# Two reorderings in an attention kernel: a small subtraction moved from VectorE to GpSimd in batch 1, and a large subtraction and its exponential moved behind two sums in five batches

## The chip, the cores and the metric

The kernel runs on one core of one Trainium2 chip. The time is the device time of one execution in microseconds (us). TensorE (PE) multiplies, VectorE (DVE) and GpSimd (POOL) do elementwise work and reductions, ScalarE (ACT) copies and takes exponentials, SyncE (SP) issues most of the DMAs. Each engine works through its own list of instructions in the order in which they were issued to it, and waits where an operand or a buffer is not ready.

## The reference, cut to what matters

All data are float32: `x` is 16 x 100 x 640, the context 16 x 722 x 384, of which the last 4 positions are the "tokens" `ca` and the other 718 are `enc`. There are 8 heads of 80.

```python
query = hidden_states @ Wq
keyt = enc @ Wk
valt = enc @ Wv
hs = _mha(query, keyt, valt)                       # large attention, 100 x 718 per head
ca_q1 = jnp.einsum('btc,th->bch', ca, Wq_ca)
ca_q1 = ca_q1[:, indices, :]
ca_hs1 = _mha(ca_q1, residual, residual)           # first softmax of the token path
ca_q2 = ca_hs1 @ Wq
ca_k2 = ca @ Wk_ca
ca_v2 = ca @ Wv_ca
ca_hs2 = _mha(ca_q2, ca_k2, ca_v2)                 # second softmax, over 4 tokens
out = hs + ca_hs2
out = out @ Wout + b_out
out = out + residual
```

## The kernel before, in words

A loop over the 16 batches `b` does, in each turn, the scores and the softmax of the large attention for batch `b`, the keys for batch `b + 1` and the values for batch `b`, the second softmax of the token path for `b`, the scores of the first softmax of the token path for `b + 1`, and the output projection of an earlier pair of row chunks. The order of all instructions on all engines is written out by hand (`tc.manual_schedule`, so the order in the source is the order on each engine).

**Keys and values.** The products of `enc` with `Wk` and `Wv` are cut into 15 products each, on sums and differences of blocks of `enc` and of the weights (class `Blocks`, lines 385 to 405; `Values`, product on line 431; `Keys`, product on line 462). `V_PLAN` and `K_PLAN` list the products: each adds into a PSUM bank (A, B, C, D or E, shown as `v_psA`, `k_psB` and so on), and after it the bank as it then stands is read into one block of the result. The first product for a block of the result is copied by ACT (line 404), every later one is added by DVE (line 402). Banks keep adding up, so the next product into a bank has to wait until the bank was read. `vv.go(n)` and `kk.go(n)` issue the next `n` values or keys products with their reads. Bank C of the values consists of two PSUM tiles, and gets the plan's products 8 and 10. Product 8 is copied by ACT; product 10 is added by DVE in two instructions of 120 x 320. `k_psC`, the bank of the keys' product 10, is opened later, in the PSUM pool that holds the two tiles of `v_psC`.

**Large softmax.** The scores lie in three tiles `st[0]` to `st[2]` of 120 x 1600. `Maximum` (lines 856 to 907) finds each row's maximum `over`; `subtract(i)` (line 1517, DVE, both inputs in SBUF) takes it off a tile and `exponential(i)` (line 1525, ACT) follows. In the middle batches the order is: values products 8 and 9, keys product 8, `subtract(0)`, `exponential(0)`, values product 10, `subtract(1)`, values 11, keys 9 and 10, `exponential(1)`, values 12, keys 11 and 12, values 13, keys 13, values 14, keys 14, `subtract(2)`, `exponential(2)`. On ACT the copy of keys product 9 (`kT<-k_psB`) thus stands behind `exponential(0)`, and on DVE the sum of values product 11 (`vs<-v_psB`) behind `subtract(1)`.

**Token path.** `scores1` (lines 972 to 990) makes the scores of the first softmax on POOL: for each of the 4 tokens a product (line 980), and from the second on an addition into `e1` (line 987). `scores2` takes two reductions on DVE (lines 1053 and 1060) and then the subtraction of the tokens' maximum, 100 x 32, on line 1062, on the engine that the caller names: DVE in batches 0 and 1, POOL in all others. `exponentials2` (1068, ACT), `softmax3` (1073 and 1074 on DVE, 1076 on POOL) and `values2` (POOL: products 1091, additions 1098; each product reads a tile `vb` that a DMA of SP fills) end the path.

**Output batches.** For `last.b in PAIRS`, that is in batches 3, 6, 8, 11 and 13, two chunks of 128 output rows are projected. `last.load` (line 1133, POOL) adds the bias onto the two tiles `xn` of the residual, `last.sums` (line 1240, POOL) forms two sums of the transposed rows, and `project_pair` does the products (line 1259, PE) and adds what they give to `xn` (line 1270, DVE); its first product is read before its bank takes the third. In the odd ones of these batches (3, 11, 13) a transposition of the token path (line 872, DVE, 128 x 800) is issued ahead of the first such read, in 6 and 8 behind it. The three tail instructions of POOL ahead of `values2` in these batches are thus: product 1076, the two sums of 1240.

Of the kernel before, what the change touches and what calls it, by code (L numbers as in the profile page):

```python
# [16 lines left out]
CAD, T = 384, 4  # L17
# [21 lines left out]
PAIRS = {ENDS[r + 1]: r for r in range(0, 10, 2)}  # L39
# [80 lines left out]
def kernel(  # L120
# [18 lines left out]
    nc = tc.nc  # L139
# [67 lines left out]
    def load_enc(b):  # L207
        enc = enc_tile(f"enc_{b}"), None
        for u, lo, hi in ((0, 0, 3), (1, 1, 3), (2, 0, 2)):
            at = A_RAW[u, lo]  # L210
            nc.sync.dma_start(
                out=enc[0][:, at : at + hi - lo],
                in_=enct[b][:, lo:hi, u * (KT - 1) : u * (KT - 1) + KT],
            )
        return enc

    def load_rest(b, enc):
        if b == 1:
            room = hsT_tile("rest_1").rearrange("p c s -> p (c s)")
            rest = room[:, : len(A_REST) * KT].rearrange("p (i k) -> p i k", k=KT)  # L220
        else:
            rest = rest_tile(f"rest_{b}")
        for (u, c), i in A_REST.items():
            nc.sync.dma_start(
                out=rest[:, i], in_=enct[b][:, c, u * (KT - 1) : u * (KT - 1) + KT]
            )
        return enc[0], rest
# [681 lines left out]
    def load_m(b):  # L909
        if b < 2:  # L910
            return lambda c: m_sb[c][:, b * HT : (b + 1) * HT]
        mb = small.tile([P, HC, HT], F32, tag="mb", name=f"mb_{b}", bufs=2)
        nc.sync.dma_start(
            out=mb, in_=m_d[:, :, b * HT : (b + 1) * HT].rearrange("c p n -> p c n")
        )
        return lambda c: mb[:, c]
# [491 lines left out]
    second = Second(0, xT, ca_0)  # L1408
# [77 lines left out]
    last, enc_next, second_next = None, load_rest(1, load_enc(1)), Second(1, xT)  # L1486
# [8 lines left out]
    for b in range(B):  # L1495
        p = b // 2
        e_in, now = enc, second
        enc, second = enc_next, second_next
# [17 lines left out]
        def subtract(i):  # L1516
            return nc.vector.tensor_tensor(  # L1517
                st[i],
                st[i],
                top.over[:KN].unsqueeze(1).to_broadcast([KN, 2, ROWS]),  # L1520
                ALU.subtract,
            )

        def exponential(i):
            nc.scalar.activation(st[i], st[i], AF.Exp, scale=SCALE)  # L1525

        def larger(i):
            for u in range(2):
                most_now = nc.vector.tensor_tensor(  # L1529
                    most[:KN], most[:KN], st[i][:, u], ALU.max  # L1530
                )
            return most_now
# [19 lines left out]
        seen = larger(2)  # L1552
# [4 lines left out]
        if b == 0:  # L1557
            second.scores1(seen)
            m_next = load_m(b + 2)
            kk.go(3)  # L1560
            top.go(3)
            first_values(3, e_in, (act, act), get=bank)
            top.go(1)
            kk.go(2)
            now.scores2()
            now.exponentials2()
            first_values(0, e_in, (act, act), (0,), bank)
            top.go()
            kk.go(3)
            first_values(0, e_in, (act, act), (1,), bank)  # L1570
            now.softmax3()
            kk.go(2)
            subtract(0)
            exponential(0)
            kk.go(2)
            subtract(1)
            kk.go(3)
            exponential(1)
            second_next, enc_next = loads()
            less = subtract(2)  # L1580
            exponential(2)
            last_keys(b + 1, enc)
            enc_next = load_rest(b + 2, enc_next)
            keys(m_next)
            now.values2(less)
            enc_sums(enc_next)
            second.softmax1(4)
        elif b + 1 < B:
            vv = Values(b, e_in)

            def both(n):
                vv.go(n)
                kk.go(n)

            forms = [wout_sb[:, 2 * i : 2 * i + 2, k * (H // 2) : (k + 1) * (H // 2)]
                     for i in range(2) for k in range(2)]
            if b == 2:
                for o, left, right in (
                    (forms[1], forms[1], forms[0]),
                    (wout2[:, 0], forms[3], forms[1]),  # L1600
                    (wout2[:, 1], forms[2], wout2[:, 0]),
                ):
                    nc.gpsimd.tensor_tensor(o, left, right, ALU.subtract)
            elif last.b - 1 in PAIRS:
                nc.gpsimd.tensor_tensor(wout2[:, 0], wout2[:, 0], forms[0], ALU.add)
            second.scores1(seen, range(T - 1))
            top.go(3)
            kk.go(3)
            vv.go(3)
            now.scores2(nc.vector if b == 1 else nc.gpsimd)  # L1610
            second.scores1(None, range(T - 1, T))
            now.load(behind=seen)
            last.load(seen)
            top.go(1)
            if b > 1:
                last.place()
            now.exponentials2()
            both(2)
            both(2)
            top.go()  # L1620
            both(1)
            now.softmax3()
            if b == 1:
                nc.gpsimd.tensor_tensor(last.hs[:S], last.hs[:S], last.hs2, ALU.add)
            if last.b in PAIRS:
                last.sums()
            later = range(T - 1, T) if b in MIXED or last.b in PAIRS else range(0)
            now.values2(None, range(T - len(later)))
            vv.go(2)
            kk.go(1)  # L1630
            subtract(0)
            exponential(0)
            vv.go(1)
            subtract(1)
            vv.go(1)
            kk.go(2)
            exponential(1)
            vv.go(1)
            kk.go(2)
            both(1)  # L1640
            both(1)
            if b == 1:
                for f in list(wv_there):
                    nc.scalar.copy(wv_sb[:, W_AT[f]], wv_there.pop(f))
            mixed = None
            if b in MIXED:
                second_next, enc_next = loads()
                mixed = Queries(p + 1, xT_at[0], enc_next[0])
                if last.b not in PAIRS:
                    mixed.sums()  # L1650
            if b == 1:
                nc.gpsimd.dma_start(out=bias, in_=bout[0].partition_broadcast(P))
            if not mixed:
                second_next, enc_next = loads()
            if b + 2 < B:
                m_next = load_m(b + 2)
            late = mixed and last.b not in PAIRS
            if not late:
                subtract(2)
            if not late and b not in PLAIN:  # L1660
                exponential(2)
            if b + 2 < B:
                enc_next = load_rest(b + 2, enc_next)
            if b == 1:
                last.transpose()
            if last.b in PAIRS:
                last.project_pair(lambda n: second.softmax1(n, True))
                if last.b == max(PAIRS):
                    nc.sync.dma_start(
                        out=forms[1],  # L1670
                        in_=wout[: 2 * P, H // 2 :].rearrange("(c p) n -> p c n", p=P),
                    )
            if not mixed and last.b in PAIRS:
                now.values2(None, later)
            if b == 1:
                second.softmax1(8)
        else:
            room = enc_tile("spare").rearrange("p f k -> p (f k)")
            spare.extend(room[:, i * H : (i + 1) * H] for i in range(2))
            last.transpose()  # L1680
            vv = Values(b, e_in)
            last.load()
            mine.load()
            now.load(behind=seen)
            top.go(3)
            vv.go(3)
            last.project_few(len(OC) - 2)
            now.scores2(nc.gpsimd)
            now.exponentials2()
            top.go(1)  # L1690
            vv.go(3)
            top.go()
            vv.go(2)
            now.softmax3()
            now.values2()
            vv.go(2)
            subtract(0)
            exponential(0)
            vv.go(5)
            for i in (1, 2):  # L1700
                subtract(i)
                exponential(i)
            last.project()
# [129 lines left out]
        last = mine  # L1833
# [55 lines left out]
```

## Time and profile before

| | before |
|---|---|
| timed runs (3) | 905.66, 906.13, 906.14 us; median 906.13 |
| profiled execution | 907.72 us, of which its span is 906.0 |
| granted TensorE clock | 1.00 |
| instructions in the span | 28486 |
| HBM traffic | 55.59 MB read, 5.57 MB written, 68 GB/s over the span |

The page of the profile gives for each engine its busy time and share; the timeline gives one row for each run of equal instructions: start and duration in us, engine, line of the kernel, operation, written tile <- read tiles with shapes, the count, and in brackets the idle time of the engine ahead of the row and what ended it. A duration of DVE or POOL holds the time that the instruction waited after it was issued. A group's row gives count, shortest, median and longest duration in ns. The waits view adds up who waited for whom (us in total, times, longest).

### The profile page before, as it was taken

Reading aid. Unit: us, or ns where it says so; the run is one execution under the profiler, and the core shown is the slowest. Engines: PE = TensorE matmul, PEld = TensorE weight load, DVE = VectorE, ACT = ScalarE, POOL = GpSimd, SP = SyncE. Lnnn points to the kernel's source line nnn. Section 1 sums busy time; section 2 is a strip of 40 time slices with the busy share of each in tenths; the row PEclk is TensorE's granted clock in tenths of the full one; section 3 lists DMA queues with packets and bytes.
Section 4 is the critical chain, followed back from the end, with each engine's and each line's share of the span. In section 5 each row is a group of like instructions: output and inputs, shape, how many; then the busy total and the mean of one; then the engine's idle time right before and its main releaser. Section 6 shows DMA issues by size and latency. Waiting matters only on the chain.

```text
span 906.0 us, 28486 instructions
## 1 busy us (share of the span) xinstructions
PE 900.3 (99%) x12200; PEld 748.1 (83%) x12200; DVE 720.6 (80%) x1278; ACT 461.9 (51%) x917; POOL 712.8 (79%) x684
## 2 busy tenths in 40 slices
PE   9999999999999999999999999999999999999998
PEld 6898889787797878878798787988879788797866
DVE  3669796999849898786987869788984899848893
ACT  2344543747437564644737446375742747437451
POOL 8689998787868889696896959958897688976633
PEclk9999999999999999999999999999999999999999
DMA  8723111132301212230122301203130031310111
GB/s 292 264 70 92 36 58 43 37 95 53 112 4 52 80 41 67 54 105 32 53 56 53 106 34 52 56 25 107 54 83 32 24 107 53 98 32 24 62 47 38
DMA packets 50627, 63.00 MB, mean 70 GB/s; under 512 B 13594, under 2 KB 37850, under 8 KB 50500
## 3 DMA queue, kind: packets, MB, share of 16 engines
q1 hardware_dynamic: 48852, 59.18, 21.4%
q8 instruction: 96, 1.57, 0.7%
q10 hardware_dynamic: 1024, 1.15, 0.4%
q0 software_dynamic: 624, 0.85, 0.3%
q14 instruction: 31, 0.25, 0.1%
HBM read 55.59 MB, written 5.57 MB: 68 GB/s over the span
## 4 chain that ended last, share of the span: by engine, by line
PE 94%; DVE 5%; ACT 0%; DMA 0%; issue 0%; DVEq 0%
PE a_ps L1806 12%; PE s_ps L781 12%; PE v_psA L431 10%; PE k_psA L462 8%; PE v_psB L431 8%; PE k_psB L462 6%; PE o_ps L1259 5%; PE k_psA L742 4%; PE v_psC L431 3%; PE k_psC L462 3%; PE v_ps L372 2%; PE q_ps L599 2%; PE q_ps L541 2%; PE v_psD L431 2%; PE v_psE L431 2%; PE k_psE L462 1%
## 5 line engine op out<-in xcount | busy, mean ns | idle before, releaser
L980 POOL TENSOR_TENSOR e<-ca,g 100x800 f32<-100x800 f32 x64 | 97.9, 1540 | 90.9 <-ACT kT L404 67.4
L1806 PEld LDWEIGHTS a_ps<-vs,st 120*64 120x64 f32 (+3 forms) x3072 | 119.0, 124 | 10.1 <-issue 0.7
L497 POOL TENSOR_TENSOR enc<-enc 128x240 f32<-128x240 f32 x144 | 113.2, 796 | 14.2 <-DMA enc<-in_enct 7.2
L1806 PE MATMUL a_ps<-vs,st 120*64 120x81 f32 (+3 forms) x3072 | 122.8, 233 | 0.0
L1517 DVE TENSOR_TENSOR st<-st,over 120x1600 f32<-120x1600 f32 x48 | 116.6, 2431 | 0.0
L431 PE MATMUL v_psA<-wv_sb,enc 128*120 128x320 f32 x352 | 109.3, 433 | 0.0
L1098 POOL TENSOR_TENSOR hs<-hs,hs 100x640 f32<-100x640 f32 x48 | 94.8, 1975 | 3.8
L987 POOL TENSOR_TENSOR e<-e,e 100x800 f32<-100x800 f32 x48 | 93.4, 1945 | 3.8
L462 PE MATMUL k_psA<-enc,wk_sb 128*128 128x240 f32 x384 | 95.2, 371 | 0.2 <-DVE kT L402 0.2
L1091 POOL TENSOR_TENSOR hs<-vb,p 100x640 f32<-100x640 f32 x64 | 90.6, 1426 | 3.8 <-DMA vb<-va_d 1.5
L431 PE MATMUL v_psB<-wv_sb,enc 128*120 128x320 f32 x296 | 91.9, 433 | 0.0
L1525 ACT ACTIVATE st<-st 120x1600 f32<-120x1600 f32 x48 | 73.9, 1539 | 23.5 <-DVE st L1517 23.2
L462 PEld LDWEIGHTS k_psA<-enc,wk_sb 128*128 128x128 f32 x384 | 71.5, 190 | 16.4 <-issue 1.2
L431 PEld LDWEIGHTS v_psA<-wv_sb,enc 128*120 128x120 f32 x352 | 64.2, 183 | 25.0 <-DVE vs L402 0.5
L1529 DVE TENSOR_TENSOR most<-most,st 120x800 f32<-120x800 f32 x64 | 68.0, 1063 | 14.3 <-ACT st L831 13.2
L462 PE MATMUL k_psB<-enc,wk_sb 128*128 128x240 f32 x320 | 77.9, 366 | 0.0
L781 PE MATMUL s_ps<-qp,kT 64*56 64x100 f32 (+1 forms) x3072 | 73.3, 248 | 0.0
L431 PEld LDWEIGHTS v_psB<-wv_sb,enc 128*120 128x120 f32 x296 | 54.1, 183 | 21.8 <-DVE vs L402 0.4
L781 PEld LDWEIGHTS s_ps<-qp,kT 64*56 64x56 f32 (+1 forms) x3072 | 67.0, 130 | 5.5 <-issue 4.2
L837 ACT COPY st<-s_ps 120x800 f32<-120x800 f32 x64 | 49.8, 830 | 38.7 <-PE s_ps L781 38.5
L1166 ACT COPY hsT<-turned_hs 32x160 f32<-32x160 f32 (+7 forms) x244 | 67.7, 278 | 3.0
L462 PEld LDWEIGHTS k_psB<-enc,wk_sb 128*128 128x128 f32 x320 | 60.9, 190 | 7.9
(213 smaller groups left out, 1905.9 us busy)
## 6 DMA issues: line engine op xcount, KB each, us to landing
vb<-va_d SPq DMA_DIRECT2D x62, 250.0 KB
enc<-in_enct SPq DMA_DIRECT2D x30, 240.0 KB
enc<-in_enct SPq DMA_DIRECT2D x15, 360.0 KB
xT<-in_xt SPq DMA_DIRECT2D x8, 500.0 KB
rest<-in_enct SPq DMA_DIRECT2D x31, 120.0 KB
xn<-in_x SPq DMA_DIRECT2D x11, 320.0 KB
out<-xn SPq DMA_DIRECT2D x11, 320.0 KB
ca<-in_cas SPq DMA_DIRECT2D x16, 156.2 KB
```

The lines of the kernel that those rows point to most:

```text
L431: nc.tensor.matmul(at[0][j][:KN, : H // 2], a_form(self.enc, f)[:, j * KN : (j + 1) * KN], wv_there.get(f, wv_sb[:, W_AT[f]]), start=first ...
L462: nc.tensor.matmul(at[:, i * KT : (i + 1) * KT], wk_sb[:, W_AT[f], i], a_form(self.enc, f), start=(first and i == 0), stop=last, skip_grou ...
L497: nc.gpsimd.tensor_tensor(out, left, right, op)
L781: nc.tensor.matmul(s_ps[at][k0:k1, cols], w, rhs, start=not begun & {(at, k) for k in range(k0, k1, 32)}, stop=last, skip_group_check=True,)
L980: first = nc.gpsimd.tensor_tensor(to, self.ca[:, t, :].unsqueeze(1).to_broadcast([S, NH, S]), g[:, :, t].unsqueeze(2).to_broadcast([S, NH, ...
L987: made = nc.gpsimd.tensor_tensor(e, e, to, ALU.add)
L1091: first = nc.gpsimd.tensor_tensor(to, self.vb[t][:S].rearrange("p (h d) -> p h d", h=NH), p2[:, :, t].unsqueeze(2).to_broadcast([S, NH, D] ...
L1098: nc.gpsimd.tensor_tensor(sums, sums, to, ALU.add)
L1517: return nc.vector.tensor_tensor(st[i], st[i], top.over[:KN].unsqueeze(1).to_broadcast([KN, 2, ROWS]), ALU.subtract,)
L1525: nc.scalar.activation(st[i], st[i], AF.Exp, scale=SCALE)
L1529: most_now = nc.vector.tensor_tensor(most[:KN], most[:KN], st[i][:, u], ALU.max)
L1806: nc.tensor.matmul(a_v[lo:hi, h % 4], st[i // 2][: KEYS[i], i % 2, h * S + lo : h * S + hi], block(i, h // 4)[: KEYS[i], h % 4], start=(i ...
```

## The change

It edits the middle branch of the loop (batches 1 to 14).

- Batch 1: `scores2` names POOL instead of DVE, and all four tokens of `second.scores1` are issued behind it. Before, three tokens were issued ahead and one behind, and the first one's explicit wait on `seen` (the third score tile's maximum, DVE) stood on the first product; this now holds only for the later batches. On POOL the 100 x 32 subtraction stands ahead of the seven instructions of `scores1`.
- Output batches (3, 6, 8, 11, 13): values product 10 with its two sums is issued ahead of `subtract(0)` and `exponential(0)` instead of behind them. PE's order and ACT's order stay as they are, since PE has nothing in `subtract` and `exponential`, and ACT has nothing in values product 10; on DVE the two sums of bank C (`vs<-v_psC`, line 402) go ahead of the first L1517, which then stands directly ahead of the second.

```diff
-            second.scores1(seen, range(T - 1))
+            if b > 1:
+                second.scores1(seen, range(T - 1))
             top.go(3)
             kk.go(3)
             vv.go(3)
-            now.scores2(nc.vector if b == 1 else nc.gpsimd)
-            second.scores1(None, range(T - 1, T))
+            now.scores2(nc.gpsimd)
+            if b > 1:
+                second.scores1(None, range(T - 1, T))
+            else:
+                second.scores1()
             now.load(behind=seen)
...
             vv.go(2)
             kk.go(1)
+            if last.b in PAIRS:
+                vv.go(1)
             subtract(0)
             exponential(0)
-            vv.go(1)
+            if last.b not in PAIRS:
+                vv.go(1)
             subtract(1)
```

## The prediction

> **What bounds the kernel now.** I read the page first (busy shares and the chain that ended last), then who TensorE waited for, then the timeline of the six places that the diff touches.
>
> ```profile
> PE 900.3 (99%) x12200; PEld 748.1 (83%) x12200; DVE 720.6 (80%) x1278; ACT 461.9 (51%) x917; POOL 712.8 (79%) x684
> ...
> PE 94%; DVE 5%; ACT 0%; DMA 0%; issue 0%; DVEq 0%
> ```
>
> ```profile
> PE k_psC L462 <- DVE vs L402: 0.3, 1, 0.3
> PE k_psA L462 <- DVE kT L402: 0.2, 1, 0.2
> ```
>
> TensorE (PE) is busy for 900.3 of 906.0 us and the chain is 94% PE. Past the start it waits in two places only, both for a sum on VectorE (DVE). So the change can give back tenths, while everything it puts late on DVE, ScalarE (ACT) or GpSimd (POOL) lengthens the run as soon as a PE product waits for it. The question is thus how much slack PE has behind the moved subtraction.
>
> **Part 1, batch 1.** The small subtraction (L1062) goes from DVE to POOL.
>
> ```profile
> 110.52 3.03 POOL L980 TENSOR_TENSOR e<-ca,g 100x800 f32<-100x800 f32 x2
> 110.83 1.28 DVE L1062 TENSOR_TENSOR e<-s,mx 100x32 f32<-100x32 f32 x1
> 114.48 1.05 PE L462 MATMUL k_psA<-enc,wk_sb 128*128 128x240 f32 x4 [0.20 <-DVE kT L402]
> 115.55 1.08 PE L462 MATMUL k_psE<-enc,wk_sb 128*128 128x240 f32 x4
> ```
>
> ```profile
> L1062 POOL TENSOR_TENSOR e<-s,mx x14: 238/243/249, 170.9 to 872.1; 100x32 f32<-100x32 f32 x14
> ```
>
> On DVE it lasts 1.28 us, ending as POOL's first product (half of 3.03) is over; on POOL the same operation takes 0.243 us. DVE gets about 1.2 us back, and its queue behind holds the sums whose lateness stopped PE for 0.20 us at 114.48. With that wait goes the slow restart behind it: k_psE follows k_psA after 1.07 us, where a key block gives way to the next after 0.81 us in batch 8 (506.67 to 507.48, quoted below). I take 0.7 us off (0.2 waited, 0.26 here, the rest in the pauses beside it), between 0.2, the wait alone, and 0.75. POOL now waits for DVE's maximum until some 110.75, so its products start about 0.45 us later, and so does what is queued behind them.
>
> ```profile
> L980 POOL TENSOR_TENSOR e<-ca,g 100x800 f32<-100x800 f32 x64 | 97.9, 1540 | 90.9 <-ACT kT L404 67.4
> ```
>
> POOL stands idle for 90.9 us ahead of such products, nearly 6 us a batch, which takes up the 0.45; without that cover it would delay batch 2's by as much.
>
> **Part 2, batches 3, 6, 8, 11 and 13.** In PE's order nothing moves; on DVE the two sums of bank C's second product go ahead of the first large subtraction (L1517), with its exponential on ACT behind. Batch 8, as it runs now:
>
> ```profile
> 498.40 3.04 POOL L1133 TENSOR_TENSOR xn<-xn,bias 128x640 f32<-128x640 f32 x2
> ...
> 499.45 3.67 DVE L1517 TENSOR_TENSOR st<-st,over 120x1600 f32<-120x1600 f32 x1
> ...
> 501.01 1.24 PE L431 MATMUL v_psC<-wv_sb,enc 128*120 128x320 f32 x4
> ...
> 503.05 0.87 DVE L402 TENSOR_TENSOR vs<-v_psC,vs 120x320 f32<-120x320 f32 x2
> ...
> 503.19 0.73 POOL L1240 TENSOR_TENSOR sum<-hsT 128x256 f32<-128x256 f32 x1
> ...
> 503.85 1.81 DVE L1517 TENSOR_TENSOR st<-st,over 120x1600 f32<-120x1600 f32 x1
> 503.97 0.97 PE L462 MATMUL k_psC<-enc,wk_sb 128*128 128x240 f32 x4
> ...
> 504.66 0.54 ACT L404 COPY kT<-k_psB 128x480 f32<-128x480 f32 x1
> ...
> 505.58 0.81 DVE L402 TENSOR_TENSOR vs<-v_psB,vs 120x640 f32<-120x640 f32 x1
> ...
> 506.20 2.50 POOL L1091 TENSOR_TENSOR hs<-vb,p 100x640 f32<-100x640 f32 x2
> ...
> 506.67 0.97 PE L462 MATMUL k_psB<-enc,wk_sb 128*128 128x240 f32 x4
> ...
> 507.48 1.24 PE L431 MATMUL v_psB<-wv_sb,enc 128*120 128x320 f32 x4
> ...
> 508.78 1.54 POOL L1098 TENSOR_TENSOR hs<-hs,hs 100x640 f32<-100x640 f32 x1
> ...
> 510.14 1.87 DVE L1517 TENSOR_TENSOR st<-st,over 120x1600 f32<-120x1600 f32 x1
> ...
> 512.58 0.49 DVE L1270 TENSOR_TENSOR xn<-o_ps,xn 128x320 f32<-128x320 f32 x1 [0.57 <-issue]
> ...
> 512.99 1.00 DVE L872 STREAM_TRANSPOSE turned<-e 128x800 f32<-128x800 f32 x1
> ...
> 513.94 1.24 PE L1259 MATMUL o_ps<-wout,hsT 128*128 128x320 f32 x4
> ```
>
> The subtraction's 3.67 us are a wait until POOL's two additions end at 501.44, and 1.69 us of work (to 503.12). Then sums, second subtraction (ends 505.65) and seven more sums follow without a gap up to the third (its turn at 510.21, 4.56 us behind the end of the second). PE's slack behind each: v_psB at 507.48 needs the sum that ends at 506.39 (1.09 us); k_psB at 506.67 needs ACT's copy that ends at 505.20 (1.47 us); the output product at 513.94 needs the read that ends at 513.07 (0.87 us).
>
> DVE and POOL exclude each other here, and whoever waits gets the next turn:
>
> ```profile
> 883.42 2.61 POOL L1091 TENSOR_TENSOR hs<-vb,p 100x640 f32<-100x640 f32 x1 [0.27 <-DMA vb<-va_d]
> 884.81 2.90 DVE L1517 TENSOR_TENSOR st<-st,over 120x1600 f32<-120x1600 f32 x1
> ```
>
> Two large subtractions stand back to back here. POOL's product, waiting since 883.42, runs between them: it ends at 886.03, having held the second up for 1.13 us past the first's end (884.90), and the second then takes 1.68 us, to 887.71. This order of DVE comes into being in the five batches by the change; today the sums lie between the subtractions, and POOL's small sum (503.19) fits beside them, since sums that read PSUM do not wait for POOL.
>
> When the moved sums can run, batch 6 shows, where the subtraction slipped in between POOL's two additions and DVE stood waiting for bank C:
>
> ```profile
> 387.09 4.64 POOL L1133 TENSOR_TENSOR xn<-xn,bias 128x640 f32<-128x640 f32 x2
> 388.33 1.99 DVE L1517 TENSOR_TENSOR st<-st,over 120x1600 f32<-120x1600 f32 x1
> 389.89 1.24 PE L431 MATMUL v_psC<-wv_sb,enc 128*120 128x320 f32 x4
> 390.63 1.03 DVE L402 TENSOR_TENSOR vs<-v_psC,vs 120x320 f32<-120x320 f32 x2 [0.30 <-PE v_psC L431]
> ```
>
> They start 0.74 us after the product and take 1.03. **Batch 8 after**, step by step:
> - Sums 501.75 to 502.78; DVE, free since some 499.5, is idle until then.
> - POOL, no longer held: its 100x32 product 0.24 (as L1062), sum 0.73, second sum of the same size 0.73, to 503.14. The subtraction comes at 502.78, waits for that, ends at 504.83 instead of 503.12.
> - ACT: exponential and the copy behind it end 2.08 us later as now, at 506.91; k_psB can start at 506.97, +0.30 us.
> - POOL's L1091 takes its 1.13 us; second subtraction 505.96 to 507.65 (+2.00). The sum of v_psB ends at 508.39: PE's v_psB at 508.45, **+0.97**.
> - Third subtraction: turn at 512.21. POOL has gone L1091 (to 508.78), L1098 (to 510.40), L1091 (to 511.74) and is in its next L1098 until 513.36. So 513.36 to 515.05, read until 515.46, output product at 515.52 instead of 513.94: **+1.58** in all.
>
> The others by the same steps:
>
> ```profile
> 222.41 3.67 DVE L1517 TENSOR_TENSOR st<-st,over 120x1600 f32<-120x1600 f32 x1
> ```
>
> ```profile
> 657.19 3.03 POOL L1133 TENSOR_TENSOR xn<-xn,bias 128x640 f32<-128x640 f32 x2
> 659.13 1.24 PE L431 MATMUL v_psC<-wv_sb,enc 128*120 128x320 f32 x4
> 662.37 1.08 PE L462 MATMUL k_psC<-enc,wk_sb 128*128 128x240 f32 x4
> ```
>
> ```profile
> 768.89 3.05 POOL L1133 TENSOR_TENSOR xn<-xn,bias 128x640 f32<-128x640 f32 x2
> 770.62 1.24 PE L431 MATMUL v_psC<-wv_sb,enc 128*120 128x320 f32 x4
> 774.08 1.08 PE L462 MATMUL k_psC<-enc,wk_sb 128*128 128x240 f32 x4 [0.34 <-DVE vs L402]
> ```
>
> - Batch 3 has batch 8's pattern (the same 3.67), but the transposition of 1.00 us stands ahead of its first read (the order for odd batches), so the read ends 1.30 us after the third subtraction: output product +2.47 (0.97 of it at v_psB).
> - Batch 6: POOL's additions end at 390.13 (387.09 plus 3.04); first subtraction 391.83 to 393.52, second ends at 396.34, v_psB +0.78, output product **+1.39**.
> - Batch 11: today k_psC comes 3.24 us after v_psC instead of 2.96 (batch 8, 501.01 to 503.97): 0.28 lost, which goes. POOL is later: first subtraction 661.12 to 662.81, then only the second sum (0.60) in between, second ends at 665.10, v_psB +0.30; the third meets an L1091, 670.43 to 672.12, output product +1.42. Net **+1.14**.
> - Batch 13: 3.46 instead of 2.96, 0.50 lost today. First 772.84 to 774.53, second ends at 776.82, v_psB +0.53, third 782.15 to 783.84, output product +1.65. Net **+1.15**.
>
> Sum: -0.7 + 2.47 + 1.39 + 1.58 + 1.14 + 1.15 = +7.0 us. No DMA moves to another place; the loads of vb wait for POOL's L1091, whose first now ends at 505.96 instead of 507.45. I take it that what follows the output products neither gives back nor adds (PE has no other waits in the trace that could shrink). The profiled execution took 907.72 us (span 906.0, 1.7 around it), 1.6 above the median 906.13 of the timed runs; I put the difference on the median: **913.2 us**.
>
> What the change adds on purpose, DVE's wait for PE ahead of the subtraction, holds up in its queue the subtractions, and behind these exponential, copy and sums; that is where the cost comes from.
>
> A rule to hold against this: the Trainium skill, "SBUF — State Buffer", section "Who interferes with whom", says that a DVE instruction with two SBUF inputs and a GpSimd instruction that reads SBUF lock each other out, and whichever issues first keeps the port pair for its whole instruction. By that rule the sum of 7.0 stands, since the L1091 was issued before the second subtraction, and the 884.81 row agrees. The 499.45 row does not: issued in POOL's first addition, the subtraction still waited out the second.
>
> **Rivals.**
> 1. *Lost turn.* As at 499.45, the first subtraction loses one more turn, now between POOL's second sum and L1091, in batches 3, 6, 8. It then starts 1.23 us later, the second ends at 508.88 in batch 8, v_psB +2.20, and the third is free by then: +0.6 each in batches 6 and 8, +0.1 in batch 3, with roundings 914.6. For it: four of five such pairs of additions. Against it: batch 6, and all other places.
> 2. *The third subtraction does not meet POOL.* Its turn depends on where POOL stands; half a microsecond either way decides. Then only v_psB's delays count: 0.97 + 0.78 + 0.97 + 0.02 + 0.03 - 0.7 = +2.1, 908.2.
> 3. *Not slower.* DVE keeps its turn through both subtractions, and finds POOL between instructions. The first then ends 3.46 us after v_psC, the second at 5.15 instead of 4.64 (batch 8): inside the slack of 1.09 and 0.87. Only the gains are left: -0.7 - 0.28 - 0.50 = -1.5, 904.6. It decides from a lateness of 1.09 us at the second subtraction. Against it: the 883 row. That the reordering does nothing is no case, as DVE's order does change.
>
> **How the numbers follow.** Forecast 0.62, lost turn 0.12, second rival 0.12, third 0.10, 0.04 for worse (two turns lost). The range 907.5 to 916.5 takes in the second rival and the lost turn, leaving out the third and the worse. Differences within 0.2% (1.8 us) can't be told from no change: the third rival lies there, as does part of the second. Slower 0.80, same 0.16, faster 0.04.
>
> **What would show it.** Right: L1517's first in the five batches starting some 1.8 us after v_psC, a POOL L1091 or L1240 between first and second, PE waits named "v_psB <- DVE vs" and "o_ps <- DVE xn", none left at the two of today. Wrong: second subtractions of 1.8 us straight behind the first, or PE still without gaps in those batches.

## The result, and the profile after

| | before | after |
|---|---|---|
| median | 906.13 us (905.66 to 906.31, 4 runs) | 916.02 us (915.29 to 916.93, 4 runs) |
| profiled execution | 907.72 us, span 906.0 | 915.29 us, span 913.6 |
| ratio | | 1.011, interval 1.0093 to 1.0128 |

The changed kernel is slower by 9.9 us, or 1.1%; the forecast was 913.2 us, with a range of 907.5 to 916.5. On the page of the changed kernel, PE's work is the same 12200 products:

```profile
span 913.6 us, 28484 instructions
...
PE 902.2 (99%) x12200; PEld 746.0 (82%) x12200; DVE 719.1 (79%) x1277; ACT 462.7 (51%) x917; POOL 708.9 (78%) x685
...
PE 94%; DVE 4%; issue 1%; DMA 0%; ACT 0%; ACTq 0%
```

Busy shares and chain tell next to nothing: the span is 7.6 us longer, and PE stays at 99%. The view of PE's waits (who waited for whom: us in total, times, longest) tells more:

```profile
PE o_ps L1259 <- DVE xn L1270: 3.6, 4, 1.3
PE v_psB L431 <- DVE vs L402: 1.6, 4, 0.4
...
PE k_psB L462 <- ACT kT L404: 0.2, 1, 0.2
```

Past the start of the run the two waits of before are gone and three new ones are there, the first two in four of the five output batches and under the names that the prediction gave. The third is listed for batch 13 alone; in the other four, TensorE waits 0.11 to 0.14 us at the same place, too short for this view. The timeline of batch 8, in order of start (where two equal instructions follow each other, a row holds both, x2):

```profile
504.44 1.24 PE L431 MATMUL v_psC<-wv_sb,enc 128*120 128x320 f32 x4
...
505.18 1.03 DVE L402 TENSOR_TENSOR vs<-v_psC,vs 120x320 f32<-120x320 f32 x2 [2.21 <-PE v_psC L431]
...
505.84 0.73 POOL L1240 TENSOR_TENSOR hsT<-sum,hsT 128x256 f32<-128x256 f32 x1
506.13 4.93 DVE L1517 TENSOR_TENSOR st<-st,over 120x1600 f32<-120x1600 f32 x2
506.53 5.67 POOL L1091 TENSOR_TENSOR hs<-vb,p 100x640 f32<-100x640 f32 x2
...
508.34 1.54 ACT L1525 ACTIVATE st<-st 120x1600 f32<-120x1600 f32 x1 [3.14 <-DVE st L1517]
...
510.38 1.08 PE L462 MATMUL k_psB<-enc,wk_sb 128*128 128x240 f32 x4
510.98 0.81 DVE L402 TENSOR_TENSOR vs<-v_psB,vs 120x640 f32<-120x640 f32 x1
511.15 1.54 ACT L1525 ACTIVATE st<-st 120x1600 f32<-120x1600 f32 x1 [0.82 <-DVE st L1517]
...
511.85 0.82 PEld L431 LDWEIGHTS v_psB<-wv_sb,enc 128*120 128x120 f32 x4 [0.77 <-DVE vs L402]
511.85 1.34 PE L431 MATMUL v_psB<-wv_sb,enc 128*120 128x320 f32 x4 [0.39 <-DVE vs L402]
...
515.26 1.54 POOL L1098 TENSOR_TENSOR hs<-hs,hs 100x640 f32<-100x640 f32 x1
515.43 3.04 DVE L1517 TENSOR_TENSOR st<-st,over 120x1600 f32<-120x1600 f32 x1
...
518.40 0.48 DVE L1270 TENSOR_TENSOR xn<-o_ps,xn 128x320 f32<-128x320 f32 x1
...
519.02 1.31 PE L1259 MATMUL o_ps<-wout,hsT 128*128 128x320 f32 x4 [0.45 <-DVE xn L1270]
```

DVE is idle for 2.21 us ahead of bank C's sums. Then the two subtractions stand back to back. Their exponentials start as each is done, at 508.34 and 511.15: 2.81 us apart, where one subtraction by itself takes 1.7. POOL's L1091, waiting since 506.53, has run between them. The sum of v_psB and the product behind it come late by that (v_psB 0.94 us: 7.41 us behind the start of v_psC's product instead of 6.47), and at 515.43 the third subtraction waits for an L1098 of POOL that ends at 516.80. In batch 3 the transposition (L872) comes on top, ahead of the read:

```profile
234.21 3.04 DVE L1517 TENSOR_TENSOR st<-st,over 120x1600 f32<-120x1600 f32 x1
...
237.17 1.00 DVE L872 STREAM_TRANSPOSE turned<-e 128x800 f32<-128x800 f32 x1
...
238.10 0.45 DVE L1270 TENSOR_TENSOR xn<-o_ps,xn 128x320 f32<-128x320 f32 x1
...
238.69 1.59 PE L1259 MATMUL o_ps<-wout,hsT 128*128 128x320 f32 x5 [1.34 <-DVE xn L1270]
```

In batch 1 the small subtraction takes 0.24 us on POOL, and both key products come without a wait, 0.81 us apart:

```profile
111.42 0.24 POOL L1062 TENSOR_TENSOR e<-s,mx 100x32 f32<-100x32 f32 x1
111.62 3.04 POOL L980 TENSOR_TENSOR e<-ca,g 100x800 f32<-100x800 f32 x2
...
114.08 0.97 PE L462 MATMUL k_psA<-enc,wk_sb 128*128 128x240 f32 x4
...
114.89 0.97 PE L462 MATMUL k_psE<-enc,wk_sb 128*128 128x240 f32 x4
```

To see what each batch costs, I took from each trace the start of each batch's first product of the scores (L781), and compared the distances from one batch to the next. Against the first profile of before, only batch 1 (-0.73 us) and the five output batches differ.

### The profile page after: what moved, and what is told of

Its sections match the earlier page's. It is cut to its first block, busy times and chain, and to the rows that moved or that the text cites. A ratio compares the mean times of both kernels' runs of the same rounds, so it can differ in the third digit from the quotient of the medians.

```text
span 913.6 us, 28484 instructions
## 1 busy us (share of the span) xinstructions
PE 902.2 (99%) x12200; PEld 746.0 (82%) x12200; DVE 719.1 (79%) x1277; ACT 462.7 (51%) x917; POOL 708.9 (78%) x685
## 4 chain that ended last, share of the span: by engine, by line
PE 94%; DVE 4%; issue 1%; DMA 0%; ACT 0%; ACTq 0%
PE s_ps L781 12%; PE a_ps L1813 12%; PE v_psA L431 10%; PE v_psB L431 8%; PE k_psA L462 8%; PE k_psB L462 6%; PE o_ps L1259 4%; PE k_psA L742 4%; PE v_psC L431 4%; DVE st L1517 3%; PE k_psC L462 2%; PE v_ps L372 2%; PE q_ps L599 2%; PE q_ps L541 2%; PE v_psD L431 2%; PE v_psE L431 2%
## 5 line engine op out<-in xcount | busy, mean ns | idle before, releaser
L980 POOL TENSOR_TENSOR e<-ca,g 100x800 f32<-100x800 f32 x64 | 99.4, 1564 | 93.0 <-ACT kT L404 78.7
L497 POOL TENSOR_TENSOR enc<-enc 128x240 f32<-128x240 f32 x144 | 112.3, 789 | 13.5 <-DMA enc<-in_enct 6.5
L1517 DVE TENSOR_TENSOR st<-st,over 120x1600 f32<-120x1600 f32 x48 | 115.5, 2417 | 0.0
L1091 POOL TENSOR_TENSOR hs<-vb,p 100x640 f32<-100x640 f32 x64 | 102.5, 1612 | 4.4 <-DMA vb<-va_d 2.0
L1098 POOL TENSOR_TENSOR hs<-hs,hs 100x640 f32<-100x640 f32 x48 | 93.2, 1943 | 3.8
L781 PE MATMUL s_ps<-qp,kT 64*56 64x100 f32 (+1 forms) x3072 | 73.1, 248 | 0.0
L781 PEld LDWEIGHTS s_ps<-qp,kT 64*56 64x56 f32 (+1 forms) x3072 | 66.9, 130 | 5.4 <-issue 4.2
```

The costliest lines, as they stand in the source:

```text
L497: nc.gpsimd.tensor_tensor(out, left, right, op)
L781: nc.tensor.matmul(s_ps[at][k0:k1, cols], w, rhs, start=not begun & {(at, k) for k in range(k0, k1, 32)}, stop=last, skip_group_check=True,)
L980: first = nc.gpsimd.tensor_tensor(to, self.ca[:, t, :].unsqueeze(1).to_broadcast([S, NH, S]), g[:, :, t].unsqueeze(2).to_broadcast([S, NH, ...
L1091: first = nc.gpsimd.tensor_tensor(to, self.vb[t][:S].rearrange("p (h d) -> p h d", h=NH), p2[:, :, t].unsqueeze(2).to_broadcast([S, NH, D] ...
L1098: nc.gpsimd.tensor_tensor(sums, sums, to, ALU.add)
L1517: return nc.vector.tensor_tensor(st[i], st[i], top.over[:KN].unsqueeze(1).to_broadcast([KN, 2, ROWS]), ALU.subtract,)
```

## The experiments

The theory is that the new order makes the subtractions late and puts them back to back, so that POOL gets a turn between them; what stands behind on DVE and ACT stops PE. There are three rivals: the first part costs something; bank C's early sums alone (DVE idle for PE) are the cost, whoever takes the turn; only the third subtraction's meeting with POOL costs. With each set of experiments the kernel before was timed again, and the ratios are against that: 906.55 us (21 runs) for e1 to e4, 906.53 (22 runs) for e5 to e8, 907.15 (21 runs) for e9 to e11. The batch losses are counted against the trace of "batch 1 only", in which PE has no wait in the loop at all. That trace takes 0.16 us longer early in batch 6 (at `z_ps`, L1021) than the two of after, so the losses of batch 6 are that much larger than they look: 1.74 us behind v_psC's product in the first profile of after.

### The two parts alone, and before once more

```diff
# e1, the second part undone in the kernel after
-            if last.b in PAIRS:
-                vv.go(1)
             subtract(0)
             exponential(0)
-            if last.b not in PAIRS:
-                vv.go(1)
+            vv.go(1)
```

The second part alone (e2) is the second block of the change, put into the kernel before.

First part alone (e1):

> Only the first part (batch 1's subtraction on POOL), the five output batches as before. Theory (the cost lies in the output batches, batch 1 gives back its wait): span 0.7 us below that of before in the same state, some 905.4 us; batch 2's scores start 0.75 us earlier, everything behind keeps its distance. Rival (POOL's later products in batch 1 cost something later, or the gain was chance): same time as before, or slower.

Second part alone (e2):

> Only the second part (the two sums of bank C ahead of the first large subtraction in the five output batches), batch 1 as before. Theory: all of the loss and 0.7 us more than the changed kernel, some 916.7 us; batches 3, 6, 8 lose 2.6, 1.6 and 1.7 us as in the changed kernel, batches 11 and 13 between 0.3 and 2 us each against before. Rival (the two parts act on each other through the places at which POOL and DVE meet): a loss under 6 us.

The kernel before, unchanged (e3):

> The kernel before, unchanged, for a second profile of it. The first profile's execution took 907.72 us against a median of 906.13. Theory: in most executions DVE's subtraction takes its turn between POOL's two additions in more of the batches than just batch 6, so that the waits of batches 11 and 13 (0.28 and 0.50 us) are not always there; the profile then shows a span of about 904.5 and fewer subtractions of 3.7 us or more. Rival: the surplus lies elsewhere (start, loads), and the subtractions look as in the first profile.

Measured: the first part 906.05 us (905.58 to 906.56; ratio 0.9993, 0.9984 to 1.0002); the second 915.77 (1.0102, 1.0088 to 1.0115); before again 906.95 (1.0002, 0.9993 to 1.0011). The loss is the second part's. The first does no harm, and can't be told from no change. Why that is so, PE's waits in the trace of before again show; past the start of the run there is this one row, for batch 13:

```profile
PE k_psC L462 <- DVE vs L402: 0.3, 1, 0.3
```

The wait for k_psA in batch 1 isn't there, though nothing was changed: batch 1 is as short in this execution (0.73 us less than in the first profile) as with the first part. POOL stood later here: its L980, which started at 110.52 in the first profile, starts behind DVE's small subtraction, and that takes 0.43 us instead of 1.28:

```profile
112.47 0.43 DVE L1062 TENSOR_TENSOR e<-s,mx 100x32 f32<-100x32 f32 x1
...
113.58 3.04 POOL L980 TENSOR_TENSOR e<-ca,g 100x800 f32<-100x800 f32 x2
```

Batch 11 is short as well (0.59 us less), as POOL's additions end 0.43 us behind the start of v_psC's product there instead of 1.09. The waits that I had counted as gains thus come and go between executions of the same kernel, with POOL's place. What I had expected of this profile did not come: the first subtraction waits out both additions in all five output batches (3.67 to 4.35 us), and the span is 906.2 us, not 904.5, since the first scores start 1.70 us later and eat up what the batches gained. I ran the first part a second time (e11) to narrow this:

> Batch 1's part alone, a second time, on the same chip as the kernel before. If batch 1's wait is there in most executions of the kernel before (0.73 us in its first profile, none in its second), the median is 0.4 to 0.7 below: ratio 0.9992 to 0.9996. If it is there only now and then, the ratio is 0.9998 to 1.0002, which cannot be told from no change.

Measured: 906.63 us (905.48 to 908.52), ratio 0.9998 (0.9989 to 1.0007). The two ratios stand for gains of 0.6 and 0.2 us; their intervals reach from 1.5 us faster to 0.6 us slower, so that no gain is shown.

### The sum of v_psB between the two subtractions

```diff
# e4, against the kernel after
             if last.b in PAIRS:
                 vv.go(1)
             subtract(0)
             exponential(0)
+            vv.go(1)
+            subtract(1)
             if last.b not in PAIRS:
                 vv.go(1)
-            subtract(1)
-            vv.go(1)
```

(In the batches that aren't output batches the result is the order of before.)

> The changed kernel, but in the output batches DVE does the sum of v_psB (values product 11) between the first and the second large subtraction. Theory (POOL's L1091 takes its turn between two subtractions that stand back to back): the sum then runs beside that L1091, the second subtraction still ends 6.64 us after v_psC, but v_psB no longer waits (its 1.0 us go) and the third subtraction's turn comes 0.7 us earlier, ahead of POOL's L1098, so that it ends 12.4 instead of 14.0 us after v_psC: 1.3 us or more back in each of batches 3, 6, 8, 11, some 910 us. Only the 0.3 us at k_psB and up to 0.8 us at the output product of the odd batches are left. Rival (DVE is late because it stood idle for bank C, whatever lies between the subtractions): v_psB waits no longer, but the output products are as late as in the changed kernel, and the time stays at 915 to 916.

Measured: 910.05 us (909.26 to 910.39), ratio 1.0036 (1.0023 to 1.005). No product waits for v_psB's sum any more, and the batches lose 0.98, 0.21, 0.37, 1.13 and 0.98 us instead of up to 2.6. So bank C's early sums by themselves are not the cost: what matters is what stands behind the second subtraction. Batch 8 here:

```profile
502.96 2.10 DVE L1517 TENSOR_TENSOR st<-st,over 120x1600 f32<-120x1600 f32 x1
503.35 5.67 POOL L1091 TENSOR_TENSOR hs<-vb,p 100x640 f32<-100x640 f32 x2
...
504.99 0.81 DVE L402 TENSOR_TENSOR vs<-v_psB,vs 120x640 f32<-120x640 f32 x1
505.72 2.15 DVE L1517 TENSOR_TENSOR st<-st,over 120x1600 f32<-120x1600 f32 x1
```

The sum runs straight behind the first subtraction, beside POOL's product, and the second's wait for POOL shrinks with it. The second still ends as late as in the kernel after (507.87, 6.6 us behind the start of v_psC's product), but PE's v_psB no longer hangs on it.

### POOL's products behind the second subtraction

The direct test of the turn (e6): everything as after, but POOL's first L1091 in the output batches is issued with a wait for the second subtraction, so it can't come between.

```diff
-            now.values2(None, range(T - len(later)))
+            if last.b not in PAIRS:
+                now.values2(None, range(T - len(later)))
...
-            subtract(1)
+            less = subtract(1)
+            if last.b in PAIRS:
+                now.values2(less, range(T - len(later)))
```

> The changed kernel, but in the output batches POOL's first product of the second softmax (L1091) waits for DVE's second large subtraction. DVE is as idle ahead of bank C as in the changed kernel, and POOL's turn between the subtractions is gone. Theory (the turn costs): second subtraction ends 5.55 us after v_psC instead of 6.64, v_psB waits no longer, 0.3 us at k_psB are left; the third subtraction's turn comes at 10.1, in or ahead of POOL's third L1091, so the output products lose 0.4 us in all in batches 6 and 8 and 1.0 to 1.4 in the odd ones: some 910 to 911 us. Rival (idle DVE alone): no better than 915.

Measured: 908.36 us (906.88 to 910.36), ratio 1.0023 (1.0014 to 1.0032); the batches lose 0.38, 0.29, 0.37, 1.41 and 0.53. Batch 8:

```profile
500.62 1.24 PE L431 MATMUL v_psC<-wv_sb,enc 128*120 128x320 f32 x4
...
502.31 3.85 DVE L1517 TENSOR_TENSOR st<-st,over 120x1600 f32<-120x1600 f32 x2
...
506.23 2.51 POOL L1091 TENSOR_TENSOR hs<-vb,p 100x640 f32<-100x640 f32 x2 [3.50 <-DVE st L1517]
...
510.53 1.81 DVE L1517 TENSOR_TENSOR st<-st,over 120x1600 f32<-120x1600 f32 x1
```

The second subtraction ends at 506.16, 5.54 us behind the start of v_psC's product instead of 6.62; the wait for v_psB is gone. It gave more than I expected, since the third subtraction no longer waits for POOL in batches 3, 8 and 13 (1.81 us instead of 3.04, as in the last row): in 3 and 13 it falls into a stretch in which POOL waits for its load of `vb` (0.32 and 0.70 us), and in batch 8 it gets its turn just as POOL's next L1091 is due. In all, 7.7 of the 9.9 us are gone with the same early sums, so these are not the cost. Not all of it is the turn between the first two subtractions: batches 6 and 11 show what that is worth by itself, since the third subtraction still waits for POOL there (2.87 and 2.86 us). They lose 1.29 and 1.22 us less than in the kernel after. So the third's meeting with POOL isn't the only cost either.

### The copy of k_psB ahead of the exponential

On top of e4 (the sum between the two subtractions), ACT copies in this experiment (e7) keys product 9 ahead of the first large exponential.

```diff
-            exponential(0)
+            if last.b not in PAIRS:
+                exponential(0)
...
-            kk.go(2)
+            kk.go(1)
+            if last.b in PAIRS:
+                exponential(0)
+            kk.go(1)
```

> The kernel with the sum of v_psB between the two subtractions, and ACT's copy of k_psB issued ahead of the first large exponential instead of behind it. Theory: the 0.1 to 0.3 us at k_psB are ACT's queue (exponential ahead of the copy), and go in all five batches; in batches 3, 11 and 13 the output product is bound by the read behind the third subtraction and comes no earlier, so only batches 6 and 8 gain, 0.2 and 0.4 us: 0.5 us under the kernel with the sum between. Rival (k_psB waits for something of DVE or POOL): its wait stays.

Measured: 909.38 us (908.87 to 910.05), ratio 1.0031 (1.002 to 1.0043). The median is 0.7 us under that of e4, but the two intervals overlap, so that this gain isn't shown by the times. In the traces, the waits for k_psB (0.07 to 0.10 us in four batches of e4) are gone in all five. From v_psC's product on, batches 6 and 8 lose 0.10 and 0.28 us less than in e4, so some of what was left there hung on ACT. Batches 3 and 11 lose as much as in e4, at the output product, and batch 13 loses 0.66 us more: POOL's additions end later there (1.18 us behind the start of v_psC's product, 0.43 in e4).

### POOL's additions moved instead

With the first part alone, POOL's two bias additions (128 x 640, for which the first subtraction waits some 2 of its 3.67 us in batch 8 before) are issued behind its two sums (e8). Seven added lines shift the line numbers here and in e10: L1517 is L1524, L1259 is L1266, L1270 is L1277, L1133 is L1140.

```diff
-        def load(self, behind=None):
+        def load(self, behind=None, late=False):
...
+                    if late:
+                        continue
                     nc.gpsimd.tensor_tensor(to, to, bias[at : at + n, cols], ALU.add)
+
+        def add_bias(self):
+
+            for xn in self.xn.values():
+                nc.gpsimd.tensor_tensor(xn, xn, bias, ALU.add)
...
-            last.load(seen)
+            last.load(seen, last.b in PAIRS)
...
                 last.sums()
+                last.add_bias()
```

> A try at a kernel that beats both: batch 1's part of the change, the output batches in the old order, and POOL's two bias additions (L1133), on which the first large subtraction waited there, issued behind its two sums (L1240). Theory: the first subtraction then starts as soon as it is issued, 1.5 us ahead of bank C's second product, and is out of the way when the sums of bank C are due; no wait at k_psC is left in any execution. Against batch 1's part alone that is 0 to 0.6 us, as the waits of batches 11 and 13 were there in some profiles only: 905.5 to 906. Rival: the additions now meet the second subtraction and hold it up by up to 1.5 us, within the slack of v_psB, or beyond it (then slower than 906.5).

Measured: 907.67 us (906.91 to 908.83), ratio 1.0013 (1.0004 to 1.0022): a miss, slower by 0.1% instead of a little faster. The first subtraction does run at once in all five batches, but the additions then hold POOL later, and its L1098 meets the third subtraction. Batch 3:

```profile
232.41 1.54 POOL L1098 TENSOR_TENSOR hs<-hs,hs 100x640 f32<-100x640 f32 x1
232.58 3.06 DVE L1524 TENSOR_TENSOR st<-st,over 120x1600 f32<-120x1600 f32 x1
...
235.56 1.00 DVE L872 STREAM_TRANSPOSE turned<-e 128x800 f32<-128x800 f32 x1
...
236.99 1.34 PE L1266 MATMUL o_ps<-wout,hsT 128*128 128x320 f32 x4 [0.44 <-DVE xn L1277]
```

The odd batches lose 0.70 each, the even ones nothing: they have no transposition ahead of the read.

### The read ahead of the transposition

So the odd batches' extra loss should be the order of two DVE instructions. I moved the read in front, once in the kernel after (e9), once in the previous experiment (e10).

```diff
             product(b1, [(one[:, :2], w(0, 0))], True)
+            read(b1, 0, 0)
             if self.b + 1 in MIXED:
                 between(1)
-            read(b1, 0, 0)
             between(1)
```

In the kernel after:

> The changed kernel, but in batches 3, 11 and 13 the read of the first output product (L1270) goes ahead of the transposition (L872, 1.00 us) on DVE instead of behind it. Theory: the odd batches lose 2.6 us and the even ones 1.6, because the third subtraction ends about as late in all five and in the odd ones the transposition stands between it and the read. So the losses of 3, 11 and 13 fall by 1.0 each: 913.0 to 913.3 us. Rival: the odd batches lose more for another reason (their token path as a whole is late behind the subtraction), and the wait only moves to a later product: 915 to 916.

With the additions moved:

> Batch 1's part alone, with GpSimd's two bias additions behind its two sums in the output batches, and the first read ahead of the transposition in batches 3, 11 and 13. With the additions moved, the three odd batches lost 0.70 us each at the output product (a gap of 0.44 at 237.11 among them) and the even ones nothing. Theory: the transposition ahead of the read is what makes the late third subtraction felt; then the 0.70 go three times, 907.7 less 2.1 = 905.6 us (905.2 to 906.0). Rival: the later reductions of the token path give the wait back, 907 to 908.

Measured: e9 914.98 us (914.26 to 916.18), ratio 1.009 (1.0076 to 1.0104); e10 907.07 (906.3 to 908.85), ratio 1.0003 (0.9995 to 1.0012). Neither theory's size came: e10 lies where its rival had it, e9 at the edge of its rival's range. In e9 the odd batches lose 2.22 to 2.24 us instead of 2.6, not 1.6. Batch 3:

```profile
236.93 0.48 DVE L1270 TENSOR_TENSOR xn<-o_ps,xn 128x320 f32<-128x320 f32 x1
...
237.33 1.00 DVE L872 STREAM_TRANSPOSE turned<-e 128x800 f32<-128x800 f32 x1
...
237.56 2.39 PE L1259 MATMUL o_ps<-wout,hsT 128*128 128x320 f32 x8 [0.44 <-DVE xn L1270]
238.36 0.99 DVE L874 TENSOR_REDUCE quad<-turned 128x25 f32<-128x800 f32 x1
239.27 0.88 DVE L1270 TENSOR_TENSOR xn<-o_ps,xn 128x320 f32<-128x320 f32 x2
...
240.20 1.34 PE L1259 MATMUL o_ps<-wout_sb,sum 128*128 128x320 f32 x4 [0.25 <-DVE xn L1270]
```

The wait at the first output product falls from 1.34 to 0.44, the same as in the even batches; but the transposition and its reduction now stand ahead of the next reads, and the product with `sum` waits for them. DVE as a whole is late there; its order mostly chooses which product feels it. In e10 the odd batches' 0.70 shrinks in the same way, to 0.39, 0.54 and 0.46.

### The kernel after, a second time

> The changed kernel, unchanged, for a second profile and more times. Theory: the losses of batches 3, 6, 8 and 11 (2.6, 1.6, 1.7, 2.0 us) return to a few hundredths, since all of them hang on positions that TensorE's own order fixes; only the start (first loads) and batch 13 differ. Rival: the turns between POOL and DVE fall otherwise from execution to execution, and batches lose other amounts than in the first profile.

Measured (e5): 916.11 us (914.37 to 917.1), ratio 1.0104 (1.009 to 1.0118). Batches 3, 6, 8 and 11 lose the same as in the first profile to 0.04 us, as expected. The trace also settles batch 13, which had lost little in the first profile of after. The first profile:

```profile
776.13 3.05 POOL L1133 TENSOR_TENSOR xn<-xn,bias 128x640 f32<-128x640 f32 x2
...
777.81 1.24 PE L431 MATMUL v_psC<-wv_sb,enc 128*120 128x320 f32 x4
...
779.50 4.52 DVE L1517 TENSOR_TENSOR st<-st,over 120x1600 f32<-120x1600 f32 x2
780.14 2.20 POOL L1240 TENSOR_TENSOR hsT<-sum,hsT 128x256 f32<-128x256 f32 x1
```

and the second, of the same kernel:

```profile
776.55 1.54 POOL L1133 TENSOR_TENSOR xn<-xn,bias 128x640 f32<-128x640 f32 x1
777.66 1.24 PE L431 MATMUL v_psC<-wv_sb,enc 128*120 128x320 f32 x4
...
779.35 4.92 DVE L1517 TENSOR_TENSOR st<-st,over 120x1600 f32<-120x1600 f32 x2
779.74 5.67 POOL L1091 TENSOR_TENSOR hs<-vb,p 100x640 f32<-100x640 f32 x2
```

POOL's additions end 1.37 us after v_psC begins in the one (779.18 less 777.81) and 0.43 in the other (778.09 less 777.66). In the first, the short second sum (L1240) gets the turn between the subtractions, in the second the longer L1091 does, as in the other four batches. What moves POOL by 0.94 us from one execution to the next was not settled.

## Why the prediction was right, and where its sizes were off

The losses by batch, in us; "predicted" is the lateness at the output product, without the gains:

| batch | predicted | after | after again |
|---|---|---|---|
| 3 | 2.47 | 2.63 | 2.59 |
| 6 | 1.39 | 1.58 | 1.56 |
| 8 | 1.58 | 1.72 | 1.71 |
| 11 | 1.42 | 2.63 | 2.66 |
| 13 | 1.65 | 0.98 | 2.59 |
| sum | 8.51 | 9.54 | 11.11 |

- **What bounds the kernel:** right. PE lost only where a product waits for a DVE sum, a DVE read or an ACT copy.
- **Batch 1:** -0.73 us against the first profile, -0.7 predicted, so the size was right for that execution. POOL's products start 1.10 us later there (111.62 instead of 110.52), not 0.45. That isn't DVE's doing: POOL itself was late, since an earlier wait of 1.14 us for a load of `vb` moved the end of its sums (L497) from 110.55 to 111.47. In e1, where these end at 110.58, the products start at 111.01, 0.49 later. Batch 2 pays nothing, so the cover held. What failed is that the wait is not in every execution of before.
- **The turn between the subtractions:** right. In batch 8 the first subtraction ends 3.82 us after the start of v_psC's product, the second 6.62, and the third 14.03 (515.43 plus 3.04); the working gives 3.82, 6.64 and 14.04. v_psB follows at 7.41 (7.44 by the working). The products-behind experiment (e6) shows that POOL's turn costs: without it the second ends at 5.54, and 1.2 to 1.3 us of the loss go even in the batches where the third subtraction still waits for POOL. By the Trainium skill, "SBUF — State Buffer", section "Who interferes with whom", whichever instruction issues first keeps the port pair for its whole length. The pairs of 4.92 to 4.98 us with an L1091 between agree, as POOL's was issued first. The 3.67 us of the first subtraction in the kernel before, which the prediction names as not agreeing, came again (3.67 to 4.35) in all five output batches of its second profile.
- **The k_psB copy:** right. In batch 8 k_psB starts 5.94 us after v_psC (5.96 by the working), 0.28 us later than before; in that batch the copy experiment (e7) takes 0.28 us off.
- **The third subtraction and its meeting with POOL:** right. Where POOL stood elsewhere and the third did not meet it, most of the loss was gone (batch 13 of the first profile, 0.98 us instead of 2.59; with the turn gone as well, batches 3, 8 and 13 of e6), as the second rival has it.
- **Batches 3 and 8:** some 0.15 us more than predicted. I had the lateness at the output product right (batch 8: 14.58 us after v_psC instead of 12.93, so 1.65 against 1.58), and nothing behind it gave it back; a little more was lost by the next scores.
- **Batch 6:** its output product comes 1.66 us late, not 1.39. I had POOL's additions end 0.24 us behind the start of v_psC's product, as in the one profile of before; in the changed kernel they end 0.45 behind it, as in batch 8.
- **Batches 11 and 13:** here the sizes were wrong. I placed POOL where the one profile of before had it, late, so that the short L1240 would come between. In the changed kernel POOL stood earlier in batch 11 in both traces, and in batch 13 in one, and the longer L1091 came between: 2.6 us instead of 1.42 and 1.65.
- **The sum on the median:** this step failed most plainly. I subtracted gains of 1.48 us (batch 1, and the waits of 11 and 13; 1.92 by the starts of the scores) that the profiled execution of before had, and put the difference on a median of executions that have them only in part: before again shows none of it in batches 1 and 11. Of the 2.9 us that were missing (9.9 measured, 7.0 forecast), batches 11 and 13 make between 0.5 (3.61 in the first trace, 3.07 predicted) and 2.2 (5.25 in the second), batches 3, 6 and 8 some 0.4 to 0.5, and the gains up to 1.5; how these fell in each timed run, no trace tells. The measured 916.02 is 0.5 us under the upper end of the range, and the room up there had been made for the lost turn, which did not come: that the range held is in part luck.
- **The rivals:** a lost turn between POOL's sum and L1091 did not come (3.82 in batch 8 excludes it); DVE never kept its turn through both subtractions, which refutes the third.

No version here is measurably faster than the kernel before. The first part alone (ratios 0.9993 and 0.9998) and e10 (1.0003) can't be told from it; all the others are slower.

## What to carry to other kernels

When two long DVE instructions that contend with POOL are put back to back, count a POOL instruction between them, and put what PE waits for (here a sum from PSUM, which can run beside POOL) between them instead. Losses that depend on where another engine stands should be worked out for its earliest and its latest place, not for the one of the single profile; and a wait of tenths that one profile shows is a gain only if a second profile of the same kernel shows it too. If several DVE instructions are late together, changing their order moves the wait to another product.

## What the runs showed of the hardware that was not expected

POOL's place moved by 0.94 us within the same batch of the same kernel (1.37 against 0.43 us behind v_psC), and with it who got the turn. And a stop of PE cost more here than the wait on its own row: ahead of v_psB in batch 8 PE's row shows 0.39 us, the weight load's 0.77, and the four products behind take 1.34 instead of 1.24. The waits of batch 8 add up to 0.95 us (0.11 for k_psB, 0.39 and 0.45), the batch lost 1.72. Where all of the remaining 0.77 us lies was not shown.
